# One GpSimd addition over four heads against four additions over one head, in an attention kernel on one core

## The chip, the cores and the metric

The kernel runs on one core of one Trainium2 chip. The metric is the time of an execution on the device in microseconds (us), as the median of several runs. The core has five engines that run side by side, each through its own queue of instructions: TensorE (PE in the profile, PEld for its weight loads), VectorE (DVE), ScalarE (ACT), GpSimd (POOL) and SyncE (SP), which here only starts transfers.

## What is computed

The input `x` has 8 sequences of 512 tokens with 128 features. The program has two parts. The first, which the change concerns, is

    x = x + Wo . attention(layernorm(x) . Wqkv)

with 16 heads of 8 features and a causal mask. Its attention is not a softmax. For each row of scores `s` a number `lam` is sought for which the weights `1 / (lam - s)` of the row sum to 1:

```python
lam = s_masked.max(-1) + 1.0
for _ in range(4):
    d = maximum(lam[..., None] - s, 1e-6)
    f = where(mask, 1 / d, 0).sum(-1) - 1.0
    fp = -where(mask, 1 / d**2, 0).sum(-1)
    lam = lam - f / fp
d = maximum(lam[..., None] - s, 1e-6)
p = where(mask, 1 / d, 0);  p = p / p.sum(-1)
```

The second part is six layers of local attention and feed-forward on the result. The change does not touch its code.

## The kernel before, in words

**Tiling.** The 512 rows of a sequence are cut into four row blocks `rb` of 128 rows; because of the mask, block `rb` needs only `W = (rb + 1) * 128` columns of scores. The 16 heads are taken as four groups `j` of four heads `g`; a tile of scores has 128 partitions and 4 heads x `W` columns.

**Steps of one row block.** `scores` (L197) multiplies queries and keys on TensorE (L204); on VectorE it turns the result into `ns`, the start of `lam` minus the score, in the memory of the core (SBUF): L209 adds the mask and takes the least value, L215 makes the start of `lam`, L217 adds it. What is left to find is how far `lam` moves from there: `dl`, one number for each row and head, 128 x 16.

`newton` (L226) is one of the four iterations, `k` from 0 to 3, for all four groups. For each it needs `ns + dl`, then the logarithm and `exp(-...)` on ScalarE, which give `1 / d`. It has three ways to add `dl`. At `k == 0` there is nothing to add (L234). For the wide blocks, `W` of 384 and 512, ScalarE adds it inside the logarithm, one head at a time (L241). For the narrow blocks, `W` of 128 and 256, GpSimd adds it for the four heads in one instruction (`add_growth`, L222), and ScalarE takes one logarithm over all (L237). L242 is the exponential. L244 on VectorE gathers mean and variance of each head, four instructions a group. Then L249 to L260, nine small VectorE instructions on 16 or 32 columns, work out the new `dl`. The tiles `d` have two buffers, so that an addition into one waits until L244 has read what was there.

`attend_add` (L262) adds the final `dl` by `add_growth` too, for every row block, wide and narrow, into a tile `da` with three buffers. `attend_weigh` (L267) takes logarithm and exponential (L269, L270) and lets GpSimd clear what lies above the diagonal (L272). `attend_sum` (L277) transposes the weights on TensorE (L286), copies them out on VectorE (L288), and multiplies them with the values (L293). `attend_end` divides, projects and adds to `x2`. `normalized_T` (L90) normalizes rows, with L103 among its VectorE instructions, and `project` (L161) makes queries, keys and values of the next sequence.

**Order.** Work items are pairs of row blocks: (3, 0) and (2, 1) of each of the 8 sequences, 16 items. The loop at the end interleaves three of them: of the last item `before` it adds and weighs a group, of the next item `nxt` it makes scores, of the item `now` it runs an iteration of `newton`. So there are 8 x 2 x 3 x 4 = 192 additions in `newton` and 8 x 4 x 4 = 128 in `attend_add`. A tile framework places the waits between engines. It also orders the instructions of each engine by a plan of its own, so that in the trace the small instructions L249 to L260 of one row block stand between the L244 of the next one, and L272 stands between additions.

A tile `ns` is written by `scores` of one item and read last by `attend_add` two steps of that loop later; L209 of the item that reuses its memory waits for that.

Of the kernel before, what the change touches and what calls it, by code (L numbers as in the profile page):

```python
# [12 lines left out]
ALU = mybir.AluOpType  # L13
# [3 lines left out]
P = 128  # L17
# [32 lines left out]
def tile_kernel(  # L50
# [18 lines left out]
    nc = tc.nc  # L69
# [41 lines left out]
    with ExitStack() as c1:  # L111
# [107 lines left out]
                )  # L219

        def add_growth(d, ns, dl, j):
            nc.gpsimd.tensor_tensor(  # L222
                d, ns, dl[:, 4 * j : 4 * j + 4].unsqueeze(2).to_broadcast(list(d.shape)), ALU.add
            )

        def newton(t, k):  # L226
            W, dl = t["W"], t["dl"]
# [2 lines left out]
            for j in range(4):  # L230
                ns = t["ns"][j]
                d = dp.tile([P, 4, W], F32, name="d", tag="d")
                if k == 0:
                    nc.scalar.activation(d, ns, AF.Ln)  # L234
                elif W <= 2 * P:
                    add_growth(d, ns, dl, j)
                    nc.scalar.activation(d, d, AF.Ln)  # L237
                else:
                    for g in range(4):
                        i = 4 * j + g  # L240
                        nc.scalar.activation(d[:, g, :], ns[:, g, :], AF.Ln, bias=dl[:, i : i + 1])  # L241
                nc.scalar.activation(d, d, AF.Exp, scale=-1.0)  # L242
                for g in range(4):
                    nc.vector.bn_stats(st[:, 4 * j + g].rearrange("p u k -> p (u k)"), d[:, g, :])  # L244
# [17 lines left out]
        def attend_add(t, j):  # L262

            d = t["d"] = dp.tile([P, 4, t["W"]], F32, name="da", tag="da", bufs=3)
            add_growth(d, t["ns"][j], t["dl"], j)
# [452 lines left out]
    while t < len(halves) * PH + LAG or parts:  # L718
        i, p = t // PH, t % PH
# [13 lines left out]
        i, c = (t + 1) // PH + 1, (t + 1) % PH  # L733
# [78 lines left out]
```

## Time and profile before

| what | value |
|---|---|
| median of 3 runs | 5671.51 us (5668.82 to 5672.67) |
| profiled execution | 5667.55 us, its span 5665.8 us |
| VectorE busy | 4786.1 us (84%) |
| TensorE busy | 4671.7 us (82%) |
| ScalarE busy | 4029.4 us (71%) |
| GpSimd busy | 3254.1 us (57%) |
| L222 into `d` (192 additions), busy | 288.4 us |
| L222 into `da` (128 additions), busy | 299.4 us |

The span runs from the first to the last instruction of one profiled execution; the execution's own time is a little longer, and it lies within 0.1% of the median. A line of a group names line, engine, operation, the tiles written and read with their shapes, and the count; then come busy time and mean length, and behind the next bar the time for which the engine stood idle just before these instructions, with what it waited for. A line of the records in order of time has start, length, engine, line, operation, tiles, and in brackets idle time before it. Times of single records are as the profiler bounds them: on one engine the next record can start a little before the last one ends.

### The profile page before, as it was taken

How to read it: one execution, taken by the hardware profiler on the slowest of the kernel's cores; microseconds unless marked ns; L12 is line 12 of the kernel's file. 1: busy time of each engine (PE TensorE's matmuls, PEld its weight loads, DVE VectorE, ACT ScalarE, POOL GpSimd, SP SyncE). 2: the span in 40 equal slices, each digit the busy share in tenths (PEclk: the TensorE clock that was granted, in tenths of full speed). 3: DMA queues.
4: the chain of work that ended last, by engine and by line, in shares of the span. 5: the costliest groups of instructions: out<-in, count | busy, mean ns of one | idle time of the engine just before them, and what ended most of it. 6: DMA issues, size and time to landing. Idle time of an engine off the chain costs nothing.

```text
span 5665.8 us, 108225 instructions
## 1 busy us (share of the span) xinstructions
PE 4671.7 (82%) x40909; PEld 2749.7 (49%) x40909; DVE 4786.1 (84%) x12028; ACT 4029.4 (71%) x6458; POOL 3254.1 (57%) x2915
## 2 busy tenths in 40 slices
PE   4556565655556549999999999999999999999998
PEld 2223232322323225666666566656665666566665
DVE  8889898998989858888888888888888888888886
ACT  5788888878888855666666666666666666666665
POOL 1333233333333337777777777777777777777774
PEclk9555555555555569999999999999999999999999
DMA  0000000000000011112111121122111211121111
GB/s 17 1 0 1 1 1 1 1 1 1 1 1 1 1 28 45 44 44 58 48 44 44 44 53 43 44 53 53 42 38 47 59 43 44 48 59 45 44 45 36
DMA packets 106559, 173.17 MB, mean 31 GB/s; under 512 B 12816, under 2 KB 30008, under 8 KB 106040
## 3 DMA queue, kind: packets, MB, share of 16 engines
q1 hardware_dynamic: 106040, 166.25, 11.8%
q8 instruction: 326, 5.34, 0.4%
q14 instruction: 193, 1.58, 0.1%
HBM read 19.42 MB, written 2.10 MB: 4 GB/s over the span
## 4 chain that ended last, share of the span: by engine, by line
PE 45%; DVE 33%; ACT 15%; POOL 5%; issue 2%; DMA 0%; SPq 0%; POOLq 0%; ACTq 0%; DVEq 0%
DVE stw L244 9%; PE m L476 8%; PE po L598 5%; PE pv L512 5%; PE pT L588 4%; PE s L559 4%; PE acc L611 3%; ACT d L241 3%; ACT d L242 3%; DVE qr L492 3%; ACT qT L540 3%; DVE ss L482 3%; PE ptq L535 3%; DVE qn L484 3%; DVE ns L209 2%
## 5 line engine op out<-in xcount | busy, mean ns | idle before, releaser
L496 POOL TENSOR_TENSOR qn<-qn,qr 128x512 f32<-128x512 f32 x768 | 976.9, 1272 | 508.3 <-DVE qr L492 359.0
L244 DVE BATCH_NORM_STATS2 stw<-d 128x6 f32<-128x512 f32 (+3 forms) x2048 | 868.3, 477 | 76.2 <-ACT d L242 74.0
L504 POOL TENSOR_TENSOR qn<-qn,ss 128x512 f32<-128x512 f32 x768 | 786.4, 1045 | 50.9 <-ACT ss L501 50.2
L578 POOL TENSOR_TENSOR pr<-pr,rs 128x768 f32<-128x768 f32 x384 | 564.8, 1471 | 386.3 <-DVE rs L577 178.0
L476 PE MATMUL m<-wqkv,xs 128*128 128x512 f32 x1536 | 740.1, 605 | 48.0 <-ACT qT L540 37.9
L482 DVE TENSOR_REDUCE ss<-sq 128x8 f32<-128x512 f32 x768 | 522.5, 680 | 289.8 <-ACT sq L481 287.0
L222 POOL TENSOR_TENSOR d<-ns,dl 128x512 f32<-128x512 f32 (+1 forms) x192 | 288.4, 1502 | 644.5 <-DVE stw L244 392.2
L242 ACT ACTIVATE d<-d 128x1536 f32<-128x1536 f32 (+3 forms) x512 | 641.3, 1261 | 5.3
L204 PE MATMUL s<-kn,qj 32*128 32x384 f32 (+3 forms) x1024 | 419.4, 751 | 245.8 <-DVE mn L209 242.6
L222 POOL TENSOR_TENSOR da<-ns,dl 128x2048 f32<-128x2048 f32 (+3 forms) x128 | 299.4, 2343 | 497.1 <-PE dTp L286 356.8
L576 DVE TENSOR_REDUCE rs<-pr 128x8 f32<-128x768 f32 x384 | 364.2, 948 | 258.0 <-ACT pr L570 258.0
L492 DVE TENSOR_TENSOR qr<-m,tab 128x256 f32<-128x256 f32 x1536 | 571.8, 413 | 0.0
L286 PE MATMUL dTp<-ident,da 128*128 128x128 f32 x1280 | 382.8, 425 | 222.1 <-ACT da L270 107.4
L481 ACT ACTIVATE sq<-m 128x512 f32<-128x512 f32 x768 | 439.4, 601 | 124.2 <-PE m L476 72.4
L605 ACT COPY oT<-po 128x512 f32<-128x512 f32 x384 | 224.2, 584 | 411.4 <-PE po L598 405.8
L484 DVE TENSOR_TENSOR qn<-m,tab 128x512 f32<-128x512 f32 x768 | 514.8, 670 | 0.0
L540 ACT COPY qT<-ptq 128x512 f32<-128x512 f32 x768 | 417.0, 583 | 86.1 <-PE ptq L535 85.4
L293 PE MATMUL po<-dT,va 128*32 128x128 f32 x2560 | 333.8, 396 | 169.8 <-DVE dT L288 169.7
L535 PEld LDWEIGHTS ptq<-ident,qn 128*128 128x128 f32 x3072 | 358.8, 141 | 224.2 <-issue 111.5
L241 ACT ACTIVATE d<-ns,dl 128x512 f32<-128x512 f32 (+1 forms) x768 | 450.6, 654 | 14.1 <-DVE stw L244 14.0
L286 PEld LDWEIGHTS dTp<-ident,da 128*128 128x128 f32 x1280 | 213.5, 203 | 479.7 <-issue 204.1
L598 PE MATMUL po<-prT,v 96*64 96x64 f32 x12288 | 443.6, 225 | 0.5 <-ACT prT L589 0.4
(137 smaller groups left out, 10083.3 us busy)
## 6 DMA issues: line engine op xcount, KB each, us to landing
v<-v SPq DMA_DIRECT2D x192, 512.0 KB
v<-v SPq DMA_DIRECT2D x96, 256.0 KB
v<-v SPq DMA_DIRECT2D x96, 192.0 KB
wqkv<-in_L_ffn_Wqkv_dram SPq DMA_DIRECT2D x36, 256.0 KB
wo<-in_L_ffn_Wo_dram SPq DMA_DIRECT2D x12, 256.0 KB
x<-in_L_attn_x_dram SPq DMA_DIRECT2D x8, 256.0 KB
out_dram<-x SPq DMA_DIRECT2D x8, 256.0 KB
w<-in_L_ffn_W_dram SPq DMA_DIRECT2D x6, 341.0 KB
```

Source lines behind the costliest of these rows:

```text
L222: nc.gpsimd.tensor_tensor(d, ns, dl[:, 4 * j : 4 * j + 4].unsqueeze(2).to_broadcast(list(d.shape)), ALU.add)
L241: nc.scalar.activation(d[:, g, :], ns[:, g, :], AF.Ln, bias=dl[:, i : i + 1])
L242: nc.scalar.activation(d, d, AF.Exp, scale=-1.0)
L244: nc.vector.bn_stats(st[:, 4 * j + g].rearrange("p u k -> p (u k)"), d[:, g, :])
L286: nc.tensor.transpose(pt[:, kb, :], d[:, g, kb * P : (kb + 1) * P], ident)
L476: nc.tensor.matmul(m.rearrange("p h e -> p (h e)"), lhsT=lhsT, rhs=wqkv[:, t, :], start=True, stop=True,)
L482: nc.vector.tensor_reduce(ss[:, t, :], sq, axis=AX.X, op=ALU.add)
L484: nc.vector.tensor_tensor(qc, m, tab[:, 2 * t, c, :].unsqueeze(1).to_broadcast([P, HH, DHL]), ALU.mult)
L492: nc.vector.tensor_tensor(qr[:, :, u, :], mh[:, :, 1 - u, :], sw.unsqueeze(1).to_broadcast([P, HH, hd]), ALU.mult,)
L496: nc.gpsimd.tensor_tensor(qc, qc, qr.rearrange("p h u e -> p h (u e)"), ALU.add)
L504: nc.gpsimd.tensor_tensor(qc, qc, ss[:, t, :].unsqueeze(2).to_broadcast([P, HH, DHL]), ALU.mult)
L598: nc.tensor.matmul(po[e * DHL : (e + 1) * DHL, n * QB : (n + 1) * QB], lhsT=g["v3"][:, n, h * DHL : (h + 1) * DHL], rhs=prT[:, e, n // 2, ...
```

## The change

In `add_growth`, one GpSimd instruction over a tile of four heads, whose second operand repeats each of four columns of `dl` along `W`, becomes four instructions over one head each, whose second operand repeats one column. Values and order of the arithmetic stay as they are. Both callers, `newton` for narrow blocks and `attend_add` for all, are changed by it.

```diff
         def add_growth(d, ns, dl, j):
-            nc.gpsimd.tensor_tensor(
-                d, ns, dl[:, 4 * j : 4 * j + 4].unsqueeze(2).to_broadcast(list(d.shape)), ALU.add
-            )
+            for g in range(4):
+                i = 4 * j + g
+                nc.gpsimd.tensor_tensor(
+                    d[:, g], ns[:, g], dl[:, i : i + 1].to_broadcast([P, d.shape[2]]), ALU.add
+                )
```

## The prediction

> **What bounds the kernel now.** I read the stretches first, then the groups by shape, the records of single instructions in order of time, the waits and the chain of waits. Stretches (length, then busy time and number of instructions of each engine, clock, DMA):
>
> ```profile
> 0.00:2110.00 2110.00, 1217.86 (x5263) 612.32 (x5263) 1843.59 (x5805) 1681.27 (x1946) 690.29 (x524) 0.58 0.01 2
> ...
> 2300.00:5665.00 3365.00, 3284.38 (x34038) 2035.99 (x34036) 2787.89 (x5897) 2237.88 (x4285) 2426.84 (x2266) 1.00 0.19 47
> ```
>
> The first part (to about 2110 us) holds every L222 addition. There VectorE is busy 1844 of 2110 us, ScalarE 1681, GpSimd only 690. The second part is TensorE's (3284 of 3365) and the change does not touch it. So GpSimd is no bound, but its additions matter in two ways. First, the groups of VectorE in the first part (busy, mean ns of one) beside one line's minimum/median/maximum:
>
> ```profile
> L257 DVE TENSOR_TENSOR sw<-sw,sw 128x16 f32<-128x16 f32 x128 | 55.9, 437 | 0.3
> L250 DVE TENSOR_TENSOR q<-q,stw 128x32 f32<-128x32 f32 x128 | 55.4, 433 | 0.0
> ...
> L259 DVE TENSOR_TENSOR sw<-sw,dl 128x16 f32<-128x16 f32 x96 | 42.4, 441 | 0.3
> ```
> ```profile
> L257 DVE TENSOR_TENSOR sw<-sw,sw x128: 141/158/2106, 68.5 to 2060.1; 128x16 f32<-128x16 f32 x128
> ```
>
> An instruction on 16 elements has a median of 158 ns and a maximum of 2106. The records in order of time (start, length) say why:
>
> ```profile
> 972.73 1.04 POOL L222 TENSOR_TENSOR da<-ns,dl 128x512 f32<-128x512 f32 x1 [4.28 <-PE dTp L286]
> ...
> 973.28 0.54 DVE L249 SCALAR_TENSOR_TENSOR q<-stw 128x32 f32<-128x32 f32 x1
> ...
> 973.73 1.89 POOL L222 TENSOR_TENSOR d<-ns,dl 128x1024 f32<-128x1024 f32 x1
> 973.75 1.91 DVE L254 TENSOR_TENSOR sw<-stw 128x16 f32<-128x16 f32 x1
> ```
> ```profile
> 1006.85 2.20 POOL L222 TENSOR_TENSOR d<-ns,dl 128x1024 f32<-128x1024 f32 x1 [0.22 <-DVE stw L244]
> ...
> 1007.18 1.91 DVE L254 TENSOR_TENSOR sw<-stw 128x16 f32<-128x16 f32 x1
> ...
> 1009.01 0.41 DVE L244 BATCH_NORM_STATS2 stw<-d 128x6 f32<-128x256 f32 x1
> ...
> 1010.93 2.07 POOL L222 TENSOR_TENSOR d<-ns,dl 128x1024 f32<-128x1024 f32 x1 [1.89 <-DVE sw L257]
> ...
> 1011.18 1.86 DVE L259 TENSOR_TENSOR sw<-sw,dl 128x16 f32<-128x16 f32 x1
> ```
>
> L254 ends 0.04 us after the addition it met, and so does L259: VectorE stands still until GpSimd's instruction is over. Second, ScalarE waits for the additions (total, times, longest):
>
> ```profile
> ACT d L237 <- POOL d L222: 226.0, 157, 5.0
> ...
> ACT da L269 <- POOL da L222: 57.4, 30, 7.8
> ```
>
> **What the Trainium skill says.** "SBUF — State Buffer", section "Who interferes with whom": VectorE and GpSimd share a port pair, held by one of them for a whole instruction; a VectorE instruction with two SBUF inputs, or in a two-port mode, blocks against a GpSimd instruction that reads SBUF; others do not. The trace agrees: L249, L250, L254, L257, L259 (two inputs) and L215, L217, L255, L260, L103 (`tensor_scalar`) are stretched, L244, L256, L288 and L209 never. "Perfetto Trace Analysis", "Optimizing Scalar/DVE Operations", says that breaking up instructions may let work finish sooner where they cause bubbles on other engines; no row here shows that for these additions. "GPSIMD Engine Reference", 3.1, has 4497 ns for an addition of 2048 elements; here one takes 3600 ns (its second operand is a broadcast), and I use the trace.
>
> **The change, part by part.** Additions by shape:
>
> ```profile
> L222 POOL TENSOR_TENSOR d<-ns,dl 128x1024 f32<-128x1024 f32 x96 | 185.1, 1928 | 282.9 <-DVE stw L244 204.4 <-ACT d L241 30.6 <-DVE sw L257 30.5
> L222 POOL TENSOR_TENSOR da<-ns,dl 128x2048 f32<-128x2048 f32 x32 | 115.2, 3600 | 46.5 <-PE dTp L286 40.1 <-DVE dl L260 5.6 <-PE pt L107 0.8
> ...
> L222 POOL TENSOR_TENSOR da<-ns,dl 128x1536 f32<-128x1536 f32 x32 | 87.9, 2747 | 74.9 <-PE dTp L286 71.4 <-DVE dl L260 3.5
> ...
> L222 POOL TENSOR_TENSOR da<-ns,dl 128x512 f32<-128x512 f32 x32 | 33.3, 1040 | 206.5 <-PE dTp L286 144.0 <-DVE dl L260 62.5
> ```
>
> Removed: 192 + 128 = 320 additions. Added: 1280. From 1040 and 3600 ns: 2560/1536 = 1.667 ns an element and 187 ns fixed (check: 1536 elements give 2747). One head of 128, 256, 384 or 512 elements then takes about 0.40, 0.61, 0.83 or 1.04 us. Two GpSimd instructions without a wait between them overlap by 0.05 us (973.73 against 972.73 + 1.04), so an addition becomes longer by 3 x (0.187 - 0.05) = 0.41 us whatever its width, 131 us in all on an engine with 1420 us to spare. No trace shows the one-head form. It could cost nothing more if its simpler access starts faster, or 0.19 us a piece (0.56 an addition) if the overlap is lost; I take 0.41. The pieces need no new wait: the first waits as the addition does now, and L237 or L269 waits for the last.
>
> *Relief on VectorE.* I counted the additions at whose end a stretched VectorE instruction ends: 154, with 205 us of waiting in all (52.8 us at 70 of 512 elements, 107.6 at 67 of 1024, 14.5 at 7 of 1536, 29.9 at 10 of 2048). Cut in four, the waiter passes at the next inner edge. Does it pass, with the next piece already queued? At 973 us it does: the second addition stands against the first, and L249 still ended between them (973.82), 0.05 us after the first. But only one passes: L254 behind it was caught by the second. So I walk VectorE's order on from each waiter: a contending instruction waits for the next edge, any other runs on at its usual step. At 1006.85 the edges fall at 1007.54, 1008.18, 1008.82 and 1009.46. L254 passes at the first, L244 takes 0.34, L250 and L255 wait for an edge each, L244 again, L252 for the last: 0.53 us gained of 1.86. At 1010.93 L259 gains 0.67 of 1.83. At 1002.41, where L215 meets the end of the addition, 0.15 is lost, since the addition ends later. The same count over all 154 gives 71 us (14.7, 39.2, 9.8 and 7.6 by shape): a third of the waiting, because L249 to L260 contend almost all. How much is on the path? In the chain of waits, taken in stretches of 100 us, the excess of those lines is 170 us of the 212 that their records hold in all: 0.8. So 0.8 x 71 = **57 us** gained.
>
> *Longer additions.* The same chain holds 41 additions of `newton` and 23 of `attend_add`: 64 x 0.41 = **26 us** lost. The other 256 lie beside VectorE or ScalarE work; if that cover goes, each costs 0.41 us. VectorE's L209 waits 26.7 us (16 times) for additions, 7 us more at most, in the 26.
>
> Sum: 57 - 26 = 31 us faster. The profiled execution took 5667.55 us (span 5665.8 and 1.75 around it): 5636.6. The median of the runs lies 4.0 above it, so 5671.5 - 31 = 5640.5. Late next after a stall goes is `newton`'s ring on two `d` buffers: addition, L237, L242, four L244.
>
> **Rivals.** (A) The forecast, chance 0.45, 5625 to 5660. (B) *ScalarE's wait decides*: once VectorE is ahead, the addition is last in the ring, and all 187 waits of ScalarE grow by 0.41: 77 us lost against 57, so 5691. It decides once more than 57/0.41 = 139 of them lie on the path; the chain shows 64, against it; that ScalarE waits 283 us for GpSimd speaks for it. 0.22. (C) *Stalls shrink with the piece*: if waiters arrive at random and meet one piece each, waiting scales with piece over addition and with the longer time held: 0.54, 0.40, 0.35 and 0.32 by shape, 205 us become 86; 0.8 x 119 - 26 = 69, so 5602. For it: many waiters are followed by L244, which never blocks; against: the walk above. 0.16. (D) Gain and loss cancel, 5671, 0.12. (E) The pieces give VectorE no way through (no relief, though the change does what it says): 26 lost and 0.8 x 154 x 0.41 = 50 more, 5747; the records at 973 us speak against it. 0.05.
>
> **How the numbers follow.** This kernel's measurement can tell about 0.2% (11 us) from no change. Faster: A and C, 0.61; same: D, 0.12; slower: B and E, 0.27. A's own range is 5625 to 5660. Eight in ten must reach over C and B: 5590 to 5700, with E and half of C's far side outside.
>
> **What would show it.** Right: 1280 records of L222 of 0.40 to 1.04 us; L254, L257 and L259 with maxima near one piece (under 1.1 us) and more of them stretched; first part near 2080 us; second part unchanged. Wrong: VectorE still stretched to 1.9 us and more (E); ScalarE's wait for L222 well above 283 us with VectorE idle (B); means of L250 to L259 below 250 ns (C). A changed order of VectorE's or GpSimd's instructions would upset the count either way.

## The result, and the profile after

| | before | after |
|---|---|---|
| median of 20 runs each, taken together | 5670.91 us | 5662.82 us (5660.75 to 5663.92) |
| profiled execution (its span) | 5667.55 us (5665.8) | 5662.83 us (5661.1) |
| VectorE busy in the first 2110 us | 1843.6 us | 1785.7 us |

The ratio is 0.9986 [0.9979, 0.9993]: 8 us faster, where 31 were forecast. The direction was right; the size was wrong by a factor of four.

The stretches of the kernel after, as before (length, then busy time and instructions of PE, PEld, DVE, ACT and POOL, clock, DMA):

```profile
0.00:2110.00 2110.00, 1198.53 (x5263) 612.50 (x5263) 1785.66 (x5806) 1681.44 (x1946) 829.57 (x1484) 0.55 0.01 3
2300.00:5665.00 3365.00, 3281.40 (x33986) 2033.38 (x33980) 2786.13 (x5894) 2235.84 (x4283) 2424.37 (x2265) 1.00 0.19 47
```

VectorE lost 58 us of busy time in the first part and GpSimd gained 139. Yet the second part's first projection (L476 before, L478 after) starts at 2114.3 us against 2115.5. So VectorE's relief is there, and almost none of it is in the time. Those 1.2 us are also less than the 8 us between the medians. From that projection to the end of the span it is 3546.8 us against 3550.3, though the change doesn't touch what runs there; in the traces of all the kernels below this stretch lies between 3545.8 and 3550.9 us. So some 5 us are the second part's own scatter, and how much of the 8 us lies in the first part is not shown. (Lines after 222 have a number higher by two now: the addition is L224, L237 is L239, L242 is L244, L244 is L246, L257 is L259.)

VectorE's small instructions by shape, and one line's minimum/median/maximum:

```profile
L252 DVE TENSOR_TENSOR q<-q,stw 128x32 f32<-128x32 f32 x128 | 28.3, 221 | 0.0
...
L261 DVE TENSOR_TENSOR sw<-sw,dl 128x16 f32<-128x16 f32 x96 | 28.7, 299 | 0.2
...
L259 DVE TENSOR_TENSOR sw<-sw,sw 128x16 f32<-128x16 f32 x128 | 27.8, 217 | 0.5
```
```profile
L259 DVE TENSOR_TENSOR sw<-sw,sw x128: 143/165/601, 68.4 to 2054.9; 128x16 f32<-128x16 f32 x128
```

The median is as it was; the maximum fell from 2106 ns to 601, one piece. The additions of the kernel after by shape:

```profile
L224 POOL TENSOR_TENSOR d<-ns,dl 128x256 f32<-128x256 f32 x384 | 226.5, 621 | 229.5 <-DVE stw L246 177.6 <-ACT d L243 30.9 <-DVE sw L259 19.2
...
L224 POOL TENSOR_TENSOR da<-ns,dl 128x512 f32<-128x512 f32 x128 | 130.9, 1052 | 44.1 <-PE dTp L288 41.7 <-DVE dl L262 2.5
L224 POOL TENSOR_TENSOR da<-ns,dl 128x384 f32<-128x384 f32 x128 | 101.7, 826 | 76.9 <-PE dTp L288 76.9
...
L224 POOL TENSOR_TENSOR da<-ns,dl 128x128 f32<-128x128 f32 x128 | 47.7, 404 | 171.4 <-PE dTp L288 137.2 <-DVE dl L262 34.2
```

A piece takes 404, 621, 826 and 1052 ns, as the line 187 + 1.667 ns an element had it (0.40, 0.61, 0.83, 1.04 us). From the first piece's start to the last one's end an addition lasts 0.45 us longer than one instruction did (mean over all 320), where I had 0.41.

The records of the kernel after in order of time show how VectorE gets past the pieces of one addition:

```profile
1002.69 2.49 POOL L224 TENSOR_TENSOR d<-ns,dl 128x256 f32<-128x256 f32 x4
1002.93 0.60 DVE L251 SCALAR_TENSOR_TENSOR q<-stw 128x32 f32<-128x32 f32 x1
1003.45 0.63 DVE L256 TENSOR_TENSOR sw<-stw 128x16 f32<-128x16 f32 x1
1004.01 0.42 DVE L246 BATCH_NORM_STATS2 stw<-d 128x6 f32<-128x256 f32 x1
1004.34 0.33 DVE L252 TENSOR_TENSOR q<-q,stw 128x32 f32<-128x32 f32 x1
1004.59 0.62 DVE L257 TENSOR_SCALAR sw<-sw 128x16 f32<-128x16 f32 x1
...
1005.22 1.06 ACT L239 ACTIVATE d<-d 128x1024 f32<-128x1024 f32 x1 [2.31 <-DVE sw L257]
```

Each contending instruction waits for one edge (the last of them for the end of the fourth piece) and passes there, L246 runs as ever: the walk of the prediction. But the last line is ScalarE's logarithm, and it begins when the fourth piece is over.

### Where the 58 us went

What VectorE itself waited for, in the first 2110 us (total, times, longest), first before, then after:

```profile
DVE stw L244 <- ACT d L242: 74.0, 69, 4.6
...
DVE ns L209 <- POOL da L222: 26.7, 16, 2.1
```
```profile
DVE stw L246 <- ACT d L244: 104.9, 124, 5.2
...
DVE ns L209 <- POOL da L224: 42.9, 15, 3.2
```

VectorE waits 31 us more for ScalarE's exponential, and nearly twice as often (124 times for 69). With its waits that the profile puts down to others, L244 (now L246) stood idle for 116.1 us against 76.2, 40 us more. VectorE waits 16 us more for the additions that read a score tile last, and 3 us more at L299 for TensorE. Together that is the 58 us, to within 1 us. VectorE no longer stands inside a blocked instruction, it stands in front of the next one. The exponential comes later because the logarithm before it does. ScalarE's records of one phase of a narrow block, first before, where the first addition starts at 1006.85, then after, where it starts at 1002.69:

```profile
1009.08 1.06 ACT L237 ACTIVATE d<-d 128x1024 f32<-128x1024 f32 x1 [2.22 <-POOL d L222]
...
1013.04 1.06 ACT L237 ACTIVATE d<-d 128x1024 f32<-128x1024 f32 x1 [1.81 <-POOL d L222]
...
1016.89 1.06 ACT L237 ACTIVATE d<-d 128x1024 f32<-128x1024 f32 x1 [1.71 <-POOL d L222]
```
```profile
1009.25 1.06 ACT L239 ACTIVATE d<-d 128x1024 f32<-128x1024 f32 x1 [1.89 <-POOL d L224]
...
1012.49 1.06 ACT L239 ACTIVATE d<-d 128x1024 f32<-128x1024 f32 x1 [1.09 <-POOL d L224]
```

Counted from that addition, the three logarithms start at 2.23, 6.19 and 10.04 us before; after, at 2.53 (1005.22, shown above), 6.56 and 9.80. First the longer addition puts the phase 0.30 and 0.37 us behind; only then does VectorE's relief bring it 0.24 ahead. Gain and loss meet on the same ring.

The table of waits hides part of this. It has 136.6 us for the logarithm's waits for additions after the change, where it had 226.0 before, because a wait is put down to whatever came last, and some now fall to VectorE's small instructions. The idle time before the logarithm as a whole, the first number behind the last bar, did grow, by 19 us:

```profile
L237 ACT ACTIVATE d<-d 128x512 f32<-128x512 f32 (+1 forms) x192 | 161.4, 841 | 226.0 <-POOL d L222 226.0
```
```profile
L239 ACT ACTIVATE d<-d 128x512 f32<-128x512 f32 (+1 forms) x192 | 161.6, 842 | 245.1 <-POOL d L224 136.6 <-DVE sw L258 51.1 <-DVE sw L259 14.8
```

### The profile page after: what moved, and what is told of

It reads as the page before. It is cut to its first block, busy times and chain, and to the rows that moved or that the text cites. A ratio compares the mean times of both kernels' runs of the same rounds, so it can differ in the third digit from the quotient of the medians.

```text
span 5661.1 us, 109651 instructions
## 1 busy us (share of the span) xinstructions
PE 4650.8 (82%) x40909; PEld 2748.7 (49%) x40909; DVE 4727.6 (84%) x12028; ACT 4028.4 (71%) x6458; POOL 3391.5 (60%) x3875
## 4 chain that ended last, share of the span: by engine, by line
PE 44%; DVE 31%; ACT 15%; POOL 6%; issue 3%; SPq 0%; DMA 0%; POOLq 0%; ACTq 0%; DVEq 0%
DVE stw L246 9%; PE m L478 8%; PE po L600 5%; PE pv L514 5%; PE s L561 4%; PE pT L590 4%; PE acc L613 3%; ACT d L244 3%; ACT d L243 3%; ACT qT L542 3%; PE ptq L537 3%; DVE qr L494 3%; DVE ss L484 3%; DVE qn L486 2%; DVE ns L209 2%
## 5 line engine op out<-in xcount | busy, mean ns | idle before, releaser
L246 DVE BATCH_NORM_STATS2 stw<-d 128x6 f32<-128x512 f32 (+3 forms) x2048 | 868.4, 477 | 116.1 <-ACT d L244 104.9
L478 PE MATMUL m<-wqkv,xs 128*128 128x512 f32 x1536 | 739.5, 604 | 47.6 <-ACT qT L542 37.6
L224 POOL TENSOR_TENSOR d<-ns,dl 128x128 f32<-128x128 f32 (+1 forms) x768 | 370.9, 514 | 556.5 <-DVE stw L246 356.2
L244 ACT ACTIVATE d<-d 128x1536 f32<-128x1536 f32 (+3 forms) x512 | 641.8, 1261 | 5.3
L224 POOL TENSOR_TENSOR da<-ns,dl 128x384 f32<-128x384 f32 (+3 forms) x512 | 356.6, 728 | 431.6 <-PE dTp L288 326.6
L204 PE MATMUL s<-kn,qj 32*128 32x512 f32 (+3 forms) x1024 | 409.6, 751 | 225.9 <-DVE mn L209 222.7
L591 ACT COPY prT<-pT 96x512 f32<-96x512 f32 x768 | 428.4, 586 | 14.6 <-PE pT L590 8.6
```

The lines of the kernel that those rows point to most:

```text
L224: nc.gpsimd.tensor_tensor(d[:, g], ns[:, g], dl[:, i : i + 1].to_broadcast([P, d.shape[2]]), ALU.add)
L478: nc.tensor.matmul(m.rearrange("p h e -> p (h e)"), lhsT=lhsT, rhs=wqkv[:, t, :], start=True, stop=True,)
```

## The experiments

The account to be tested: VectorE's relief is as forecast, and the longer additions cost far more than 26 us, because ScalarE waits for the last piece also where VectorE stood blocked. In the expectations S is the account in which this wait of ScalarE decides, and V the one in which VectorE's own work sets the pace. N is the one in which gain and loss net differently by width or caller, O the one in which VectorE's relief lies off the path. A further rival, P, is that the changed order of instructions ate the gain: told apart by line and tiles, 4658 of VectorE's 5798 records in the first part stand at the place in the sequence that they had before, and 1887 of ScalarE's 1944.

All results, each against runs of the kernel before on the same chip. "Order held" is explained below. Gains and losses in us are differences of these medians; by the ratio, which some of the expectations use, they come out up to 3 us apart.

| run | median us | before us | ratio [95%] |
|---|---|---|---|
| e1_mid | 5664.8 | 5671.1 | 0.9988 [0.9980, 0.9996] |
| e2_ends | 5663.9 | 5671.1 | 0.9987 [0.9980, 0.9993] |
| e3_newton | 5660.5 | 5671.1 | 0.9982 [0.9975, 0.9990] |
| e4_attend | 5660.9 | 5671.1 | 0.9984 [0.9978, 0.9991] |
| e6_delay | 5754.2 | 5668.3 | 1.0146 [1.0130, 1.0162] |
| e7_nolock | 5576.6 | 5668.3 | 0.9835 [0.9816, 0.9854] |
| e8_act | 5534.9 | 5668.3 | 0.9759 [0.9741, 0.9777] |
| e9_dve | 5710.1 | 5668.3 | 1.0070 [1.0053, 1.0087] |
| p1_after, order held | 5664.5 | 5673.5 | 0.9984 [0.9976, 0.9991] |
| p2_delay, order held | 5734.0 | 5673.5 | 1.0102 [1.0087, 1.0118] |
| p3_nolock, order held | 5602.2 | 5673.5 | 0.9871 [0.9853, 0.9888] |
| p5_dve, order held | 5618.8 | 5673.5 | 0.9900 [0.9885, 0.9915] |
| p4_act, order held | 5657.8 | 5670.2 | 0.9977 [0.9968, 0.9987] |
| p6_halves, order held | 5662.7 | 5670.2 | 0.9985 [0.9978, 0.9992] |
| p7_ln4, order held | 5645.9 | 5670.2 | 0.9955 [0.9942, 0.9967] |
| p8_ln2, order held | 5641.6 | 5670.2 | 0.9946 [0.9932, 0.9959] |
| p9_buf3, order held | 5685.9 | 5671.1 | 1.0025 [1.0016, 1.0033] |
| p10_buf3_after, order held | 5636.7 | 5671.1 | 0.9937 [0.9925, 0.9950] |

### One part of the change alone

e1_mid cuts only the additions with `W` of 256 and 384, e2_ends those of 128 and 512; e3_newton only the calls in `newton`, e4_attend only those in `attend_add`.

The width `n` of a piece in heads is set by this line in e1_mid (in e2_ends it has `(P, 4 * P)`); in e3_newton and e4_attend it is a parameter, which one caller gives as 1 and the other as 4.

```diff
-            nc.gpsimd.tensor_tensor(
-                d, ns, dl[:, 4 * j : 4 * j + 4].unsqueeze(2).to_broadcast(list(d.shape)), ALU.add
-            )
+            n = 1 if d.shape[2] in (2 * P, 3 * P) else 4
+            for g in range(0, 4, n):
+                i = 4 * j + g
+                nc.gpsimd.tensor_tensor(
+                    d[:, g : g + n], ns[:, g : g + n],
+                    dl[:, i : i + n].unsqueeze(2).to_broadcast([P, n, d.shape[2]]), ALU.add
+                )
```

> Only the additions of the row blocks with W of 256 and 384 (work items (2, 1)) are cut in four; those of 128 and 512 stay whole. Theory N (relief and length nearly cancel, by width): the whole change moved items (2, 1) by about -1.6 us each and items (3, 0) by about +1.5 us each, so this one gives 8 x -1.6 = -13 us, ratio 0.9977. Theory O (VectorE's relief lies off the path, something else sets the pace): within 5 us of before, ratio 0.999 to 1.001. Theory P (the framework's changed order of instructions decides): any value, and this and e2_ends do not add up to the change's -8 us.

> Only the additions of the row blocks with W of 128 and 512 (work items (3, 0)) are cut in four. Theory N: slower than before, 8 x +1.5 = +12 us less the 4 us that the first items gained, ratio 1.0010 to 1.0020. Theory O: within 5 us of before. Theory P: any value; e1_mid and this do not add up to -8 us.

> Only the 192 additions of newton are cut in four, the 128 of attend_add stay whole. Theory N: these meet most of the waiting (about 160 of 205 us) and all 157 of ScalarE's waits of L237, so most of the -8 us should be here, ratio 0.998 to 1.000. Theory O: within 5 us of before. Theory P: this and e4_attend do not add up to -8 us.

> Only the 128 additions of attend_add are cut in four. Theory N: they are the longest (2.7 and 3.6 us), and little waits for them but L269 and L209, so the relief is nearly free: ratio 0.997 to 0.999. Theory O: within 5 us of before. Theory P: this and e3_newton do not add up to -8 us.

Measured: each of the four gains 6 to 11 us. They don't add up: by width 6 and 7 (together 13 to 14), by caller 11 and 10 (together 20 to 21), the whole 8. Each has an interval of about 4 us to either side, so only the sum by caller stands clear of the whole. So no width or caller holds a large gain that another spends, and N, which had one half of the widths faster and the other slower, fell. What one half brings, the other doesn't bring again; this is what P expected too, and it was left standing.

### Costs alone, the order left free

e6_delay leaves the additions whole and puts a fill of 108 columns a head ahead of each, so that the addition comes later.

```diff
         def add_growth(d, ns, dl, j):
+            nc.gpsimd.memset(d[:, :, 0:108], 1.0)
```

e7_nolock replaces the addition by fills, which read nothing.

```diff
-            nc.gpsimd.tensor_tensor(
-                d, ns, dl[:, 4 * j : 4 * j + 4].unsqueeze(2).to_broadcast(list(d.shape)), ALU.add
-            )
+            nc.gpsimd.tensor_tensor(d[:, :, 0], ns[:, :, 0], dl[:, 4 * j : 4 * j + 4], ALU.add)
+            nc.gpsimd.memset(d[:, :, 1:], 1.0)
+            nc.gpsimd.memset(d[:, :, 32:], 1.0)
```

e8_act leaves out a quarter of each wide exponential (95 us of ScalarE in all), e9_dve a quarter of the columns of each wide L244 (119 us of VectorE).

```diff
-                nc.scalar.activation(d, d, AF.Exp, scale=-1.0)
+                h = 3 if W > 2 * P else 4                    # e8_act
+                nc.scalar.activation(d[:, 0:h], d[:, 0:h], AF.Exp, scale=-1.0)
...
-                    nc.vector.bn_stats(st[:, 4 * j + g].rearrange("p u k -> p (u k)"), d[:, g, :])
+                    n = W * 3 // 4 if W > 2 * P else W       # e9_dve
+                    nc.vector.bn_stats(st[:, 4 * j + g].rearrange("p u k -> p (u k)"), d[:, g, 0:n])
```

> The kernel before, with a fill of 432 elements of d (estimated 0.41 us, from fills of 128 and 512 elements at 0.205 and 0.526 us, less the overlap) on GpSimd ahead of each of the 320 additions, which then write over it: each addition ends 0.41 us later, as in the change, and gives VectorE no way through. Theory V (the prediction: 64 additions lie on the path): +26 us, ratio 1.0045. Theory S (ScalarE runs close behind VectorE and waits for about 100 additions in earnest): +40 to +65 us, 1.007 to 1.0115. If all 187 waits of ScalarE grow: +77 us, 1.0135.

> Leaves out the addition but for the first column of each head: the rest of d is filled with 1.0 by two fills, so that GpSimd is occupied about as long as by the addition (0.19 us of addition, then fills that read nothing). Waits on dl, ns and buffers stay. VectorE's instructions with two inputs (135 of its 212 us of excess) should no longer be held, the tensor_scalar ones perhaps still. Theory V (0.8 of VectorE's excess is on the path): 108 to 170 us faster, ratio 0.970 to 0.981. Theory S (ScalarE is next in line at once): 30 to 60 us faster, 0.989 to 0.995.

> The kernel before with 95 us taken off ScalarE in the first part: for the wide row blocks (W of 384 and 512) newton's exponential covers three of the four heads (256 instructions shorter by 0.32 or 0.43 us); the fourth head's exponential is left out. Theory V (VectorE's path sets the pace): at most 20 us faster. Theory S (ScalarE sets it in the wide phases): 60 to 95 us faster, ratio 0.983 to 0.990.

> The kernel before with about 119 us taken off VectorE in the first part: for the wide row blocks L244 reads three quarters of the columns (512 instructions shorter by 0.133 us, 512 by 0.1); the last quarter is left out of the sums. Theory V: 0.8 x 119 = 95 us faster, ratio 0.983. Theory S: VectorE's time in the wide phases lies beside ScalarE's, 0 to 30 us faster, 0.995 to 1.000.

Measured: +86, -92, -133 and +42 us. e8_act gained more than the work taken off, and e9_dve became slower with 119 us less to do. Neither can be the price of that work. The traces suggest why: the framework had planned another order. Of VectorE's 5798 records in the first part only 1787 stand in e9_dve at the place that they had before, in e8_act 1358. So these four say nothing certain on the costs, and the change itself came under suspicion.

### The change with the order held

From here on each engine's instructions are tied to the order of the kernel before, by ordering edges that wait for nothing; pieces that are added stand next to the instruction that they belong to. p1_after is the change in that order. In its trace all 5798 of VectorE's and 1944 of ScalarE's records in the first part stand where they stood before. No run holds the order and changes nothing else. (The lines of these kernels have numbers higher by 80 to 87: in p1_after L290 is L209, L305 is L222, L327 is L242, L329 is L244.) The diffs after this one leave out the marks (`tail`) that tie added pieces to their place.

```diff
+                one = nc.gpsimd.tensor_tensor(
+                    d[:, g], ns[:, g], dl[:, i : i + 1].to_broadcast([P, d.shape[2]]), ALU.add
+                )
+                if g:
+                    tail.add(one.ins.name)
...
+    follow_plan(tc, tail, fore)
```

> The change, with the order of the instructions of TensorE, VectorE, ScalarE and GpSimd held to that of the kernel before (edges of order between neighbours; each group of four additions stands where its one addition stood). Theory V (the prediction): 31 us faster, ratio 0.9945. Theory S (ScalarE close behind VectorE; gain and loss nearly cancel): as the change itself, 5 to 15 us faster, 0.9975 to 0.999. Theory P (the new order of instructions ate the gain): 25 to 45 us faster, 0.992 to 0.9955.

Measured: -9 us, as with the order free. The order is not the cause. What is stretched in VectorE's instructions fell from 212 to 138 us. (I count what each record lies above the lower quarter of its like, where that is over 60 ns.) The waits again take it back:

```profile
DVE stw L329 <- ACT d L327: 109.1, 115, 5.6
...
DVE ns L290 <- POOL da L305: 38.9, 16, 2.8
```

VectorE's wait for the exponential is 35 us above that of before, that for the additions 12.

### Later additions, and additions that block less

p2_delay has the edit of e6_delay, p3_nolock that of e7_nolock (it leaves the addition out but for one column a head); both with the order held.

> e6_delay (a fill of about 0.41 us ahead of each of the 320 additions) with the order held to that of before. Theory V (64 additions on the path): +26 us, ratio 1.0045. Theory S (about 100 of them wait in earnest): +40 to +65 us, 1.007 to 1.0115. If e6_delay's +83 us were a matter of order, this shows it by being far from that.

> e7_nolock (additions replaced but for one column by fills as long, which read nothing; the sums are left out) with the order held to that of before. Theory V (0.8 of VectorE's excess on the path): 0.8 x the excess that goes (at least 58 us in e7_nolock), so 50 us or more faster, up to 108 if all two-input waiting goes. Theory S: 20 to 50 us faster.

p2_delay lost 60 us (interval 49 to 67), in the range of S. The fill is longer than meant. GpSimd's records in order of time, and the fills as a group:

```profile
1033.47 0.46 POOL L303 MEMSET d<- 128x432 f32 x1 [5.46 <-DVE stw L326]
1034.01 1.89 POOL L304 TENSOR_TENSOR d<-ns,dl 128x1024 f32<-128x1024 f32 x1
...
1038.42 0.72 POOL L303 MEMSET d<- 128x432 f32 x1 [0.20 <-DVE stw L326]
1039.23 1.93 POOL L304 TENSOR_TENSOR d<-ns,dl 128x1024 f32<-128x1024 f32 x1
```
```profile
L303 POOL MEMSET d<- 128x432 f32 x190 | 92.1, 485 | 592.1 <-DVE stw L326 429.2 <-DVE lam L296 76.4 <-ACT d L323 29.9
```

From a fill's start to its addition's start it is 0.54 us in most pairs (1033.47 to 1034.01). So 60 us are 111 additions' worth; the 64 that the prediction counted would give 35. Fills also block: VectorE's stretching rose by 12 us, which by the prediction's factor of 0.8 accounts for up to 10 of the 60. Then 50 / 0.54 = 93 additions are left. At the 0.45 us by which the change lengthens one, 93 to 111 of them come to 42 to 50 us.

p3_nolock gained 71 us, in the range of V. Its stretching by the count above fell by 49 us in all (212 to 163): the two-input instructions gave up nearly all of theirs (135 to 11 us), the `tensor_scalar` lines took some on (77 to 121), and 31 us stand in lines that had none, L244's above all. One line of each of the first two kinds:

```profile
L338 DVE TENSOR_TENSOR sw<-sw,sw x128: 143/163/535, 68.3 to 1995.4; 128x16 f32<-128x16 f32 x128
...
L298 DVE TENSOR_SCALAR ns<-ns,lam x512: 192/407/1989, 29.5 to 1839.9; 128x512 f32<-128x512 f32 x43, 128x384 f32<-128x384 f32 x43, 128x256 f32<-128x256 f32 x43, 128x128 f32<-128x128 f32 x42
```

The 31 us are the same time counted again. L244 (here L325) is not held by the fill; its records lie behind a `tensor_scalar` that is, and all end with it:

```profile
883.60 1.80 POOL L304 MEMSET da<- 128x2044 f32 x1
...
883.90 1.59 DVE L184 TENSOR_SCALAR xn<-x,mv,rstd 128x128 f32<-128x128 f32 x1
884.25 1.25 DVE L325 BATCH_NORM_STATS2 stw<-d 128x6 f32<-128x128 f32 x4
```

With time under several records counted once, stretching fell by 92 us (210 to 118), and the gain is 0.77 of that. Blocking is thus worth money on the path, and the prediction's 0.8 fits. (The fills last 0.09 us longer than the addition that they replace, so a little more may be lost in them.)

### What sets the pace in the wide phases

p4_act is e8_act and p5_dve is e9_dve with the order held; they leave out what those leave out.

> e8_act (the exponential of the wide row blocks leaves out one head of four: 95 us off ScalarE) with the order held to that of before. Theory S2 (ScalarE runs without a gap through the wide phases and is the pace there): 60 to 95 us faster, ratio 0.983 to 0.990. Theory V (VectorE's path): at most 20 us faster. If e8_act's 134 us were partly a matter of order, this is less.

> e9_dve (L244 of the wide row blocks over three quarters of the columns, the rest left out of the sums; 119 us off VectorE) with the order held to that of before. Theory V: 0.8 x 119 = 95 us faster, ratio 0.983. Theory S: 0 to 30 us faster, 0.995 to 1.000. If e9_dve's +40 us came from its order, it is gone here.

Measured: 12 us for 95 us of ScalarE, 55 for 119 us of VectorE. ScalarE's own work in the wide phases hardly matters, and V was right there. For VectorE's 119 us neither account was: V had 95, S at most 30. The first 2000 us, kernel before and then p4_act:

```profile
0.00:2000.00 2000.00, 1173.91 (x4954) 587.80 (x4958) 1782.67 (x5625) 1617.30 (x1872) 645.13 (x484) 0.57 0.01 2
```
```profile
0.00:2000.00 2000.00, 1172.29 (x4991) 585.96 (x4991) 1785.83 (x5654) 1535.07 (x1888) 645.69 (x484) 0.55 0.01 2
```

ScalarE is busy 82 us less and the other engines as before. What ScalarE no longer does, it waits: p4_act's narrow logarithms waited 269.6 us for additions, where those of before waited 226.0. A lengthening therefore doesn't act through ScalarE's load in the wide phases. That leaves the narrow phases, where each addition, logarithm, exponential and L244 follow one another.

### Fewer pieces, and an earlier logarithm

p6_halves cuts each addition in two instead of four.

```diff
+            for g in (0, 2):
+                i = 4 * j + g
+                nc.gpsimd.tensor_tensor(
+                    d[:, g : g + 2], ns[:, g : g + 2],
+                    dl[:, i : i + 2].unsqueeze(2).to_broadcast([P, 2, d.shape[2]]), ALU.add
+                )
```

p7_ln4 has the four pieces of the change, p8_ln2 the two of p6_halves, and both cut the narrow logarithm in two, so that its first half need not wait for the last piece.

```diff
-                    nc.scalar.activation(d, d, AF.Ln)
+                    nc.scalar.activation(d[:, 0:2], d[:, 0:2], AF.Ln)
+                    nc.scalar.activation(d[:, 2:4], d[:, 2:4], AF.Ln)
```

> Each addition cut in two over two heads instead of four over one, order held to that of before. Lengthening 0.14 instead of 0.41 us an addition. Theory S2 (the change is relief of about 69 us, p1_after against p2_delay, less a lengthening of about 58 us, p2_delay): lengthening 20 us; the prediction's walk with two pieces gives 25 us of relief instead of 71: 5 us faster, ratio 0.9985 to 1.000. Theory V (0.8 of the relief, 64 additions on the path): 20 - 9 = 11 us faster. If relief follows the longest piece alone (half of all waiting): 0.5 x 205 - 20 = 80 us faster.

> The change (four pieces) and, in newton, ScalarE's logarithm L237 cut in two over two heads each, so that it starts when two pieces are there; order held. Theory S2 (ScalarE's wait for the last piece is what takes the gain back, at about 135 of 187 additions): after the last piece half a logarithm is left instead of a whole one, 0.27 us (W of 128) to 0.43 us (W of 256) sooner, at an estimated 0.1 us more of ScalarE each: 25 to 45 us faster than the change, ratio to before 0.990 to 0.994. Theory V (few additions on the path): within 10 us of the change, or slower by 192 x 0.1 = 19 us.

> Additions cut in two, and L237 cut in two with them, order held. Theory S2: 5 us from the halves and 25 to 45 us from the earlier logarithm: ratio 0.991 to 0.995. Theory V: 11 us from the halves, less up to 19 us for the second logarithm: 0.998 to 1.002.

p6_halves gains 7 us, about what four pieces do: less relief (stretching 212 to 176), a smaller lengthening (0.14 us). With the earlier logarithm the same pieces gain 24 (p7_ln4, 15 more than p1_after) and 29 (p8_ln2, 21 more than p6_halves). p8_ln2 lies where S2 had it; p7_ln4 falls short of S2's 25 to 45 and is more than V's 10. VectorE's wait for the exponential, in p6_halves, p8_ln2 and p7_ln4:

```profile
DVE stw L330 <- ACT d L328: 83.3, 81, 5.0
```
```profile
DVE stw L331 <- ACT d L329: 66.8, 70, 4.7
```
```profile
DVE stw L330 <- ACT d L328: 90.7, 91, 5.6
```

The earlier logarithm takes 17 us off this wait with two pieces (83.3 to 66.8, below the 74.0 of before) and 18 with four (109.1 in p1_after to 90.7, half of what the change had added), beside gains of 21 and 15. This is the loss of the change seen from its other end: give the logarithm a start before the last piece, and part of that wait is back. The edit adds ScalarE work (a second instruction for 192 logarithms, 38 us in all) and gains all the same. It is also what the Trainium skill, "Perfetto Trace Analysis", section "Optimizing Scalar/DVE Operations", says may happen when an instruction that causes bubbles elsewhere is broken up: here it is ScalarE's, with 21 us beside it.

### A looser ring

p9_buf3 gives the `d` tiles of group 2 in the narrow blocks a buffer of their own, to loosen the ring on two buffers; to make room the transposed weights have four buffers instead of five and `o` and `oT` one instead of two. p10_buf3_after is that with the change.

```diff
-        tr = c1.enter_context(tc.tile_pool(name="tr", bufs=5))
+        tr = c1.enter_context(tc.tile_pool(name="tr", bufs=4))
...
-                d = dp.tile([P, 4, W], F32, name="d", tag="d")
+                own = W <= 2 * P and j == 2
+                d = dp.tile([P, 4, W], F32, name="d", tag="dn" if own else "d", bufs=1 if own else 2)
...
-            o = bt.tile([P, H, DH], F32, name="o")
+            o = bt.tile([P, H, DH], F32, name="o", bufs=1)
...
-            oT = bt.tile([P, P], F32, name="oT")
+            oT = bt.tile([P, P], F32, name="oT", bufs=1)
```

> The kernel before, order held, with a buffer of its own for the third group's tile d of newton's narrow row blocks, so that its addition and the fourth's no longer wait for the sums (L244) of the tile two groups back. To make room, dT has four buffers instead of five, o and oT one instead of two. Theory R (in the narrow phases the ring addition, logarithm, exponential, L244 on two buffers sets the pace, and the lengthening acts through it): 10 to 60 us faster than before, unless the smaller buffers take it back. If the ring is not what counts: within 10 us of before or slower.

> The change on top of p9_buf3 (same buffers, order held). Theory R: with the ring loosened the 0.41 us of each addition is mostly hidden and the relief on VectorE stays, so this is 25 to 60 us faster than p9_buf3, against 9 us with two buffers. If the lengthening acts elsewhere (the first addition of a phase, which waits for no buffer): this is 0 to 20 us faster than p9_buf3, as with two buffers.

p9_buf3 is 15 us slower than the kernel before, where R had it faster unless the smaller buffers took that back. p10_buf3_after is 34 us faster, the fastest of the versions that leave no work out. Between the two the change is worth 49 us instead of 9, in the range of R. One line's extremes in both, p9_buf3 first:

```profile
L339 DVE TENSOR_TENSOR sw<-sw,sw x128: 142/158/2106, 69.4 to 2076.5; 128x16 f32<-128x16 f32 x128
```
```profile
L343 DVE TENSOR_TENSOR sw<-sw,sw x128: 146/170/597, 68.3 to 2025.0; 128x16 f32<-128x16 f32 x128
```

But stretching fell from 254 to 147 us here, by 107 instead of 74: there was more to free, I suppose because with a third buffer more additions run beside VectorE's small instructions. By the factor of 0.8 that is 86 us, and 86 - 49 = 37 us of loss remain. So the third buffer makes the gain larger; how far it also hides the lengthening is not shown. Nor did I separate what makes p9_buf3 slow, the smaller buffers or the additional blocking.

## Why the prediction was right or wrong

**The relief on VectorE held.** The walk gave 71 us of waiting that goes; 62 went (212 to 150), and 74 with the order held. The pattern in the records is the walk's, and the maxima are one piece. Times 0.8, which p3_nolock's 0.77 supports, that is 50 and 59 us, against 57 forecast. Rival E (no way through) fell with the records, C (119 us of waiting gone) with the sum, though two of its lines (L250, L257) do have means below 250 ns.

**The step that failed** is "Longer additions": "64 x 0.41 = **26 us** lost. The other 256 lie beside VectorE or ScalarE work". The 0.41 us were nearly right (0.45; the overlap given as 0.05 us is 0.04 in the records shown, which alone makes it 0.44). The 64 were not. The loss is 42 to 50 us, from two sides: relief less net gain, 50 - 8 = 42 and 59 - 9 = 50; and p2_delay's count at 0.45 us, 42 to 50. That is 93 to 111 additions in earnest. (If of the gain only what the first part shows in the traces is taken, 1.2 us and 0.1 in p1_after, the first side gives 49 and 59.)

The chain of waits itself, followed once more in the later traces, says the same. In the first part it holds 64 additions before (41 of `newton`, 23 of `attend_add`), 104 after the change (59 and 45), 117 with the order held (71 and 46), and 105 in p2_delay (66 and 39). So the cover of the 256 went for 40 to 53 of them as soon as the additions became longer, and the count from the trace before could not show it.

My reading of why: the chain follows one releaser at each step. Where VectorE stood blocked until an addition's end, it went on through VectorE's record, and the addition didn't appear in it. Yet ScalarE's logarithm may wait for the same end. Cut in four, the addition lets VectorE go early and ScalarE later than before. The walk moved the first waiter and left the second where it was. In the trace before, 89 additions are of this kind, not on the chain themselves: it runs through a stretched VectorE record at their end, and ScalarE waits for that end too; 88 of them are `newton`'s. With the order held the additions can be compared one by one: 63 are new on the chain, at the end of 33 of these it ran through a stretched VectorE record before, and at 18 ScalarE waited as well. So the reading fits a part of the new ones. How the others came onto the chain, 23 of `attend_add` among the 63, stays open. That the late logarithm costs is shown, by VectorE's wait for the exponential (+31, +35 us) and by p7_ln4 and p8_ln2, which win back 15 and 21 us; for the rest of the loss the waits and the chain speak, and no run separates it.

**"Late next"** was named rightly (addition, L237, L242, four L244) and priced at nothing. It was the place: L244's wait for L242. L209's additional wait was put at 7 us at most and is 16, with the order held 12.

**Rival B** had this mechanism with all 187 waits of ScalarE, 77 us. The runs show a little over half of it, so its point (more than 139 additions on the path) was not reached. Its sign in the profile was given as ScalarE's wait for L222 grown well above 283 us. In the table of waits that sum fell to 197.5 us, for the reason given above, and the logarithm's idle time grew by only 19; what grew most was VectorE's wait for ScalarE. Rival D, gain and loss that cancel, came nearest in time: 8 us lie within the 0.2% called no change. That the measured time lies within the wide range (5590 to 5700 us) is owed to the room left for the rivals: A's own range ended at 5660.

**The first part** was to end near 2080 us and hardly moved, which follows from the above.

## What to carry to other kernels

When an instruction is cut into pieces, list every engine that waits for its end, not only the one that the chain of waits passes through: whoever can use an inner edge gains, whoever needs the last piece loses. Cut the latter's instruction too: two pieces with the logarithm in halves gave 29 us where two or four pieces alone gave 7 to 9. A count of what lies on the chain holds for the trace that it was read from; here it went from 64 to over 100 with the edit. And where a framework orders the instructions, hold the order before a single cost is measured: the same edits gave -133 and +42 us with it free, -12 and -55 with it held.

## What was not expected of the hardware

- A waiting VectorE instruction gets past at the edge between two queued GpSimd instructions, at three inner edges in a row in the records from 1002.69 us on; the prediction had one such case to go by.
- A GpSimd instruction that only writes still holds VectorE's `tensor_scalar`: in p3_nolock L217's stretching rose from 22.9 to 55.7 us with a maximum of 1989 ns, while two-input instructions came free (2106 to 535 ns). The Trainium skill, "SBUF — State Buffer", section "Who interferes with whom", has both halves of that: two inputs contend only with a GpSimd instruction that reads, two-port modes with either. The prediction's summary had put one condition on both. The trace agrees, if these `tensor_scalar` run in such a mode, which the profile doesn't tell.
- The same fill took 0.46 us in one place and 0.72 in the next (p2_delay); no run separates why.
